# Keys of the first batch in halves, constants in an early gap, and the first token sums on VectorE

## The chip, the cores and the metric

The kernel runs on one core of one Trainium2 chip. The core has four engines that compute, each with its own queue of instructions in program order: TensorE (PE in the profile, its weight loads apart as PEld) multiplies matrices into PSUM, VectorE (DVE) and ScalarE (ACT) work on tiles in SBUF and PSUM, and GpSimd (POOL) works on tiles in SBUF alone. SyncE (SP) only issues transfers. The metric is device time in microseconds, the median over runs; one further execution is recorded by the profiler.

## The reference

The input x has eight batches of 1024 tokens with 512 features. A layer norm without weights gives xn. From it come two things that are multiplied and added back to x:

```python
xn = _layernorm(x)
s = concat([local, sparse, memory, prediction]) @ warboss_w + warboss_b
g = silu(relu(xn @ w1 + b1) @ w2 + b2)          # 512 -> 2048 -> 512
return x + s * g

# local:   softmax(q k^T * scale) v, one head of 128
# sparse:  the same, but a row keeps only its k_sparse = 102 largest of 1024 scores
#          (kth = top_k(scores)[..., -1]; where(scores >= kth, scores, -1e9))
# memory:  xp = xn @ memory_proj_w; weights = softmax(xp bank^T); [xp, weights bank] @ mem_out_w + b
# prediction: three linear layers, a gelu behind the second
```

All of it is in 32-bit floats.

## The kernel before, in words

A batch is cut into eight tiles of 128 tokens, four pairs, and two groups of 512 tokens. Token tiles are normalized with tokens in rows and turned by TensorE (`turn_tokens`, L328) into `xnT`, features in rows, one tile of 128 x 4 x 512 per group. For each tile of queries, `local` (L820) and `sparse` (L885) multiply the queries with the 1024 keys (`scores`, tile names `sc`), make a softmax, turn the probabilities (`ptp`) and, for a pair at a time, multiply with the values (`pa`). In `sparse` VectorE finds the 102nd largest score of each row in 13 rounds of MAX8 and MATCH_REPLACE8 (`sparse_select`, L850); ScalarE then scales the exponentials `es` by the reciprocal `r_s`.

The large products (both layers of the feed-forward, the two projections of the side heads, later queries and keys, and the output product) are made with seven block products where eight would be plain, as Strassen and Winograd do: sums of blocks of one operand (`t`, made from `xnT` in `token_sums`, L535; `hs` and `ho` from hidden values and heads), sums of blocks of the weights (`form_chunk`, L487), seven products, and sums of these (`u_...`, `m`). Weights are formed once, written back to DRAM and read from there afterwards.

The order of instructions on every engine is fixed when the kernel is built. `InOrder` (L77) chains each engine's instructions as the Python code issues them. The code keeps a model clock in units of TensorE columns (`clock`, L108): `run` (L133) looks through the chains, generators that yield the model time or the condition at which they may go on, takes the first that is ready, and otherwise issues one more multiplication of the feed-forward (`filler`, L662). `start` (L158) adds a chain with a rank. So a step that is issued at another place, or with another cost, shifts the model clock for what is behind it, and the planner may then order later steps in another way.

PSUM is shared by `ring` (L190): four buffers that are taken in turn; a buffer comes free when ScalarE has copied it out.

The change touches the first batch. `first_tokens` (L1043) normalizes eight tiles, two, two and four at a time, turns them, and makes the keys of the sparse head for one group of 512 tokens at a time (`project_k`, L342: four multiplications of 512 columns, one copy). After the first group come the first queries (`project_q`, L375), and three chains are started: `turn_constants` (L272), which turns the bias rows and the memory bank and multiplies the bank with half of `mem_out_w`; `token_sums` for group 0, four sums on GpSimd; and `hidden_sums`. Chunk 0 of the weights is formed by VectorE after the first four tiles are turned and the next four normalized. Then `sparse(0, 0)` multiplies the first scores; `run(needs(("sparse scores", 0)))` (L1071) waits for that, and queries of the second pair and the keys of the local head follow. From there a loop over 64 tiles sets the pace.

Of the kernel before, what the change touches and what calls it, by code (L numbers as in the profile page):

```python
# [15 lines left out]
P = 128  # L16
# [4 lines left out]
def kernel(  # L21
# [30 lines left out]
    NT = S // P  # L52
    NP = NT // 2
    NG = NT // 4
    T = 2 * P
    ND = D // P
# [7 lines left out]
    LOCAL, SPARSE = 0, 1  # L64
# [12 lines left out]
    class InOrder:  # L77
# [23 lines left out]
    pe, act, dve, pool, sp = (  # L101
        InOrder(e) for e in (nc.tensor, nc.scalar, nc.vector, nc.gpsimd, nc.sync)
    )
# [20 lines left out]
    def on(engine, columns):  # L124
        clock[engine] = max(clock[engine], clock["pe"]) + columns

    def after(engine, more=SLACK):
        return clock[engine] + more
# [29 lines left out]
    def start(generator, due=0, rank=1):  # L158
        chains.append([due, generator, rank])
        chains.sort(key=lambda c: c[2])  # L160

    def matmul(out, lhsT, rhs, start, stop, columns):
        pe.matmul(out, lhsT, rhs, start=start, stop=stop)
        tick(columns)

    def transpose(out, in_, ident):
        pe.transpose(out, in_, ident)
        tick(P // 2)

    def accumulate(ps, lhs, rhs, columns):  # L170
        n = len(lhs)
        for c in range(n):
            matmul(ps, lhs[c], rhs[c], c == 0, c == n - 1, columns)

    def copy(out, ps, columns):
        act.copy(out, ps)
        on("act", columns)

    def on_pool(op, out, in0, in1):
        getattr(pool, op)(out, in0, in1)  # L180
        n = 1
        for d in out.shape[1:]:
            n *= d
        on("pool", 60 + int(1.42 * n))

    def on_dve(op, out, in0, in1):
        getattr(dve, op)(out, in0, in1)
        on("dve", 340)

    def ring(name, shape):  # L190
        return ps_r.tile(list(shape), F32, tag="r", name=name)
# [32 lines left out]
    def borrow_qkv(name, which, tag="ws"):  # L224
        return borrow(name, *[w[:, which * HD : (which + 1) * HD] for w in qkv], tag=tag)
# [3 lines left out]
    first_k = borrow_qkv("wk_0", 1, "el")  # L229
    for h in range(2):  # L230
        t = sb.tile([P, 2, D], F32, tag="s", name=f"xl_0_{h}", bufs=2)
# [3 lines left out]
    first_q = borrow_qkv("wq_0", 0)  # L235
# [10 lines left out]
    for v in (ffn_b1, mem_out_b, pred_in_b, pred1_b, pred2_b):  # L246
        n = v.shape[0] // P
# [24 lines left out]
    def turn_constants():  # L272
        pt = ring("pt_b", (P, 4, P))
        transpose(pt[:, 0, :NB], brow, ident[:NB, :NB])
        transpose(pt[:, 1, :M], bank, ident[:M, :M])
        act.copy(biasT, pt[:, 0, :NB])
        copy(bankT[:, :M], pt[:, 1, :M], 300)
        yield after("act")
        pt = ring("pt_bm", (P, P))
        matmul(pt, bankT, w_mo[:, 1, :], True, True, HD)  # L280
        copy(bank_mo, pt, 200)
        done.add("constants")


    done = set()
    stats = {}
    xnT = {}
    qT = {}
    kT = {}
    vv = {}  # L290

    def needs(*keys):
        return lambda: all(k in done for k in keys)

    def ln_stats(b, j, t):
        if j == 0:
            mv = small.tile([P, NT, 2], F32, tag="mv", name=f"mv_{b}")
            rs = small.tile([P, NT], F32, tag="rs", name=f"rs_{b}")
            stats[b] = (mv, rs)
        st = small.tile([P, 6], F32, tag="st", name=f"st_{b}_{j}")  # L300
        dve.bn_stats(out=st, in_=t)
        dve.bn_aggr(out=stats[b][0][:, j, :], in_=st)
        on("dve", 540)
# [34 lines left out]
    def make_k(b):  # L338
        if b not in kT:
            kT[b] = sb.tile([P, 2, S], F32, tag="kT", name=f"kT_{b}")  # L340

    def project_k(b, g, h, w):  # L342

        make_k(b)
        ps = ring(f"pk_{b}_{g}_{h}", (P, 512))
        accumulate(
            ps,
            [w[:, c, ts(h, HD)] for c in range(ND)],
            [xnT[b, g][:, c, :] for c in range(ND)],
            512,  # L350
        )
        copy(kT[b][:, h, ts(g, 512)], ps, 360)
        done.add(("k", b, g, h))

    def project_v(b, q, w):

# [12 lines left out]
    def pair_xnT(b, p):  # L369
        return [xnT[b, p // 2][:, c, ts(p % 2, T)] for c in range(ND)]  # L370

    def make_q(b, p):
        qT[b, p] = sb.tile([P, 2, T], F32, tag="qT", name=f"qT_{b}_{p}", bufs=2)

    def project_q(b, p, w):  # L375

        make_q(b, p)
        ps = ring(f"pq_{b}_{p}", (P, 2, T))
        for h in range(2):
            accumulate(  # L380
                ps[:, h, :], [w[:, c, ts(h, HD)] for c in range(ND)], pair_xnT(b, p), T
            )
        act.activation(qT[b, p], ps, AF.Copy, scale=SCALE)
        on("act", 360)
        done.add(("q", b, p))
# [101 lines left out]
    def form_chunk(at):  # L487

        if at not in raw:
            return  # L490
        kind, n, k = order_of_chunks[at]
        what = raw.pop(at)
        w = w_tiles[kind, n, k]
        if what in ("down", "po"):
            on = on_pool if what == "down" else on_dve
            on("tensor_sub", w[:, 5], w[:, 3], w[:, 0])
            on("tensor_sub", w[:, 2], w[:, 6], w[:, 5])
            on("tensor_sub", w[:, 3], w[:, 6], w[:, 3])
            on("tensor_sub", w[:, 4], w[:, 1], w[:, 2])
        else:  # L500
            on_dve("tensor_add", w[:, 5], w[:, 3], w[:, 4])
            on_dve("tensor_sub", w[:, 2], w[:, 5], w[:, 0])
            on_dve("tensor_sub", w[:, 3], w[:, 0], w[:, 3])
            on_dve("tensor_sub", w[:, 6], w[:, 1], w[:, 2])
        sp.dma_start(out=w_dram[what, k], in_=w)
# [29 lines left out]
    def token_sums(g, name):  # L535

        b, q = divmod(g, NG)
        if g:
            yield needs(*[("xnT", b, 4 * q + j) for j in range(4)])
            yield after("act", 0)  # L540
        t = sb.tile([P, 4, 2, T], F32, tag="t", name=f"t_{name}")
        xs = xnT[b, q]
        b11, b12, b21, b22 = (xs[:, ts(h, 2), ts(j, T)] for h in range(2) for j in range(2))
        on_pool("tensor_sub", t[:, 0], b12, b11)
        on_pool("tensor_sub", t[:, 1], b22, t[:, 0])
        on_pool("tensor_sub", t[:, 2], b22, b12)
        on_pool("tensor_sub", t[:, 3], b21, t[:, 1])
        yield after("pool")
        tokens[g] = (b11, b21, t[:, 1], t[:, 2], t[:, 3], t[:, 0], b22)

    SLOTS = ((1, 4), (6, 5))
# [65 lines left out]
    def left_sums(h1, h2, s):  # L617


        a11, a21, a12, a22 = (h[:, ts(j, P)] for h in (h1, h2) for j in range(2))  # L620
        on_pool("tensor_add", s[:, 0], a21, a22)
        on_pool("tensor_sub", s[:, 1], s[:, 0], a11)
        on_pool("tensor_sub", s[:, 2], a11, a21)
        on_pool("tensor_sub", s[:, 3], a12, s[:, 1])
        return (a11, a12, s[:, 1], s[:, 2], a22, s[:, 0], s[:, 3])

    def hidden_sums():

        for _, n, k in [c for c in order_of_chunks if c[0] == "down"]:
            yield lambda: (n, k) in hidden and sums_made[0] < downs_made[0] + 3  # L630
            yield after("act", 0)
            h = hidden.pop((n, k))
            s = sb.tile([P, 4, P], F32, tag="hs", name=f"hs_{n}_{k}", bufs=3)
            operands[n, k] = left_sums(h[:, 0], h[:, 1], s)
            sums_made[0] += 1
            due = after("pool")
            wanted_at[n, k] = due
# [405 lines left out]
    def first_tokens():  # L1043
        def normalize_tokens(j0, j1):
            for j in range(j0, j1):
                ln_stats(0, j, first_x[j])
            ln_rstd(0, j0, j1)
            return [ln_apply(0, j, first_x[j]) for j in range(j0, j1)]

        due = normalize_tokens(0, 2) + normalize_tokens(2, 4)  # L1050
        for at in range(3):
            load_chunk(at)
        for g in range(NG):
            for j in range(4 * g, 4 * g + 4):
                yield due[j]
                turn_tokens(0, j, first_x[j])
            if g == 0:
                due += normalize_tokens(4, 8)
                form_chunk(0)
            yield after("act", 200)  # L1060
            project_k(0, g, SPARSE, first_k)
            if g == 0:
                project_q(0, 0, first_q)
                start(turn_constants())
                start(token_sums(0, 0), rank=0)
                start(hidden_sums(), rank=-1)

    STEP = int(0.995 * (11775 + NWC * (2 * 7 * T + 2 * 7 * H) // 4))
    start(first_tokens())
# [4 lines left out]
    for g in range(NG):  # L1074
        project_k(0, g, LOCAL, first_k)
# [3 lines left out]
    for n in range(B * NT):  # L1079
        b, i = divmod(n, NT)  # L1080
        p = i // 2
# [56 lines left out]
```

## Time and profile before

| | us |
|---|---|
| median of three runs | 2895.06 |
| the three runs | 2895.06, 2892.13, 2895.14 |
| the profiled execution's own time | 2892.31 |
| its span, first to last instruction | 2890.3 |
| TensorE busy | 2848.1 |
| VectorE busy | 2376.7 |
| GpSimd busy | 2187.9 |
| ScalarE busy | 1672.6 |
| mean granted TensorE clock | 0.997 |

The page gives busy time by engine, groups of instructions, and what ended the idle time before them. Further views show instructions in order of time (start, duration, engine, operation, output <- inputs, shapes, count; in brackets the idle time before and what ended it), who waited for whom, and the busy time of every engine in chosen stretches, in the order PE, PEld, DVE, ACT, POOL, with the clock that TensorE was granted (1.00 is full), the share of the transfer engines and GB/s. One 32-bit multiplication appears as two passes. Nearly all lines name L85, the helper that issues each instruction, so tile names tell steps apart.

### The profile page before, as it was taken

What the parts mean: (1) busy time and instruction counts of PE and PEld (TensorE: products, weight loads), DVE (VectorE), ACT (ScalarE), POOL (GpSimd) and SP (SyncE); (2) the same over time, 40 slices, a digit from 0 to 9 for tenths busy, and PEclk for the clock granted to TensorE, in tenths of its full rate; (3) what the DMA queues carried; (4) which work ended last, traced back from release to release, by engine and by line L of the source; (5) the groups of instructions that cost most, each with busy time, mean ns of one, the idle gap of its engine ahead of it and who ended that gap; (6) DMA issues with size and microseconds to landing.
All of it is one profiled execution on the core that took longest, in us unless ns stands there. A gap on an engine that the chain in (4) does not pass through costs nothing. (4 is left out here: it accounts for less than half of the span.)

```text
span 2890.3 us, 38499 instructions
## 1 busy us (share of the span) xinstructions
PE 2848.1 (99%) x13296; PEld 2394.5 (83%) x13296; DVE 2376.7 (82%) x3202; ACT 1672.6 (58%) x3174; POOL 2187.9 (76%) x2908
## 2 busy tenths in 40 slices
PE   8989999999999999999999999999999999999998
PEld 6878888888888888888888888888888888887887
DVE  7999979878698785988769897789967989588696
ACT  3546556665566654656546665556655556465564
POOL 4787867868678696786958879587796887867785
PEclk9999999999999999999999999999999999999999
DMA  5665644655455454454545545455455554544545
GB/s 179 215 243 193 209 160 160 223 179 205 148 178 214 175 201 162 172 213 163 206 165 186 206 177 193 164 204 199 156 196 184 186 203 169 197 146 174 200 168 187
DMA packets 132001, 538.89 MB, mean 186 GB/s; under 512 B 13790, under 2 KB 40432, under 8 KB 131808
## 3 DMA queue, kind: packets, MB, share of 16 engines
q1 hardware_dynamic: 126352, 519.23, 50.7%
q0 software_dynamic: 5456, 17.22, 1.6%
q8 instruction: 105, 1.72, 0.2%
q14 instruction: 88, 0.72, 0.1%
HBM read 500.35 MB, written 36.04 MB: 186 GB/s over the span
## 5 line engine op out<-in xcount | busy, mean ns | idle before, releaser
L85 DVE MAX8 top<-left 128x8 f32<-128x1024 f32 x768 | 943.2, 1228 | 26.7
L85 POOL TENSOR_TENSOR u_up<-u_up 128x256 f32<-128x256 f32 (+1 forms) x640 | 620.8, 976 | 318.7 <-ACT u_up L85 293.9
L85 DVE MATCH_REPLACE8 left<-top,left 128x1024 f32<-128x1024 f32 x704 | 850.6, 1208 | 0.0
L85 PE MATMUL f<-w_down,hs 128*128 128x256 f32 x2048 | 539.0, 380 | 2.1 <-POOL w_down L85 1.7
L85 PE MATMUL ph_up<-t,w_up 128*128 128x256 f32 x2048 | 483.3, 379 | 0.1
L85 PEld LDWEIGHTS f<-w_down,hs 128*128 128x128 f32 x2048 | 383.6, 191 | 61.5 <-issue 9.2
L85 PEld LDWEIGHTS ph_up<-t,w_up 128*128 128x128 f32 x2048 | 383.1, 190 | 60.2 <-issue 12.0
L85 PE MATMUL f<-w_down,h 128*128 128x256 f32 x1536 | 421.7, 380 | 3.4 <-ACT h L85 3.4
L85 ACT COPY u_up<-ph_up 128x512 f32<-128x512 f32 (+1 forms) x512 | 265.5, 531 | 237.8 <-PE ph_up L85 237.2
L85 PE MATMUL ph_up<-xnT,w_up 128*128 128x256 f32 x1536 | 383.1, 380 | 1.4 <-ACT u_up L85 0.9
L85 POOL TENSOR_TENSOR hs<-h 128x128 f32<-128x128 f32 x512 | 241.4, 471 | 171.2 <-PE f L85 135.7
L85 PEld LDWEIGHTS f<-w_down,h 128*128 128x128 f32 x1536 | 288.3, 191 | 50.7 <-issue 9.6
L85 PEld LDWEIGHTS ph_up<-xnT,w_up 128*128 128x128 f32 x1536 | 288.0, 190 | 48.8 <-issue 8.8
L85 PE MATMUL sc<-kT,qT 128*128 128x512 f32 x512 | 240.4, 593 | 0.2 <-ACT el L85 0.2
L85 PE MATMUL pa<-pT,v 128*128 128x256 f32 x1024 | 231.6, 379 | 0.0
L85 ACT ACTIVATE h<-u_up,biasT 128x256 f32<-128x256 f32 x512 | 220.2, 501 | 14.1 <-POOL u_up L85 14.1
L85 DVE TENSOR_REDUCE nml<-el 128x1 f32<-128x1024 f32 x64 | 77.3, 1208 | 181.0 <-ACT el L85 180.8
L85 PEld LDWEIGHTS pa<-pT,v 128*128 128x128 f32 x1024 | 194.4, 190 | 28.1 <-issue 1.0
L85 DVE MAX8 top<-s 128x8 f32<-128x1024 f32 x64 | 78.2, 1223 | 167.7 <-ACT s L85 167.5
L85 ACT COPY pT<-ptp 128x512 f32<-128x512 f32 x256 | 149.5, 588 | 113.7 <-PE ptp L85 113.1
L85 ACT ACT_TABLE_LOAD x139 | 178.3, 1283 | 5.0 <-DVE nms L85 2.0
L85 POOL TENSOR_TENSOR u_po<-u_po 128x256 f32<-128x256 f32 (+1 forms) x155 | 146.4, 951 | 19.8 <-ACT u_po L85 13.4
(151 smaller groups left out, 4574.7 us busy)
## 6 DMA issues: line engine op xcount, KB each, us to landing
w_down<-w_down_dram SPq DMA_DIRECT2D x248, 896.0 KB, 4.7
w_up<-w_up_dram SPq DMA_DIRECT2D x120, 896.0 KB, 4.6
w_po<-w_po_dram SPq DMA_DIRECT2D x62, 896.0 KB, 4.6
xl<-in_L_attn_x_dram SPq DMA_DIRECT2D x64, 256.0 KB, 4.8
xr<-in_L_attn_x_dram SPq DMA_DIRECT2D x64, 256.0 KB, 5.0
out_dram<-xr POOLq DMA_DIRECT2D x62, 256.0 KB, 3.0
xs<-in_L_attn_x_dram SPq DMA_DIRECT2D x56, 256.0 KB, 4.9
w_q<-w_q_dram SPq DMA_DIRECT2D x15, 896.0 KB, 4.6
```

The lines of the kernel that those rows point to most:

```text
L85: r = made(*args, **kwargs)
```

## The change

`project_k` can make a part of a group: with `parts=2` it multiplies 256 columns at a time and copies 256 columns of keys; the group counts as done with its last part. In `first_tokens` the loop goes over pairs of tiles, and a half projection follows each pair. `turn_constants` is no longer a chain of its own: its transposes are issued behind the first pair of tiles, its product behind the first half projection. The normalization of tiles 4 to 7 is issued behind that, the chains of token sums and hidden sums and the first queries behind the second pair, and chunk 0 is formed behind the third. `token_sums` issues group 0's four sums on VectorE, those of all other groups on GpSimd as before. The local head's keys and all other batches call `project_k` or make keys as before.

```diff
-    def project_k(b, g, h, w):
+    def project_k(b, g, h, w, part=0, parts=1):
 
         make_k(b)
-        ps = ring(f"pk_{b}_{g}_{h}", (P, 512))
+        n = 512 // parts
+        ps = ring(f"pk_{b}_{g}_{h}_{part}", (P, n))
         accumulate(
             ps,
             [w[:, c, ts(h, HD)] for c in range(ND)],
-            [xnT[b, g][:, c, :] for c in range(ND)],
-            512,
+            [xnT[b, g][:, c, ts(part, n)] for c in range(ND)],
+            n,
         )
-        copy(kT[b][:, h, ts(g, 512)], ps, 360)
-        done.add(("k", b, g, h))
+        copy(kT[b][:, h, ts(parts * g + part, n)], ps, 360 // parts)
+        if part == parts - 1:
+            done.add(("k", b, g, h))
...
-        on_pool("tensor_sub", t[:, 0], b12, b11)
-        on_pool("tensor_sub", t[:, 1], b22, t[:, 0])
-        on_pool("tensor_sub", t[:, 2], b22, b12)
-        on_pool("tensor_sub", t[:, 3], b21, t[:, 1])
-        yield after("pool")
+        on = on_pool if g else on_dve
+        on("tensor_sub", t[:, 0], b12, b11)
+        on("tensor_sub", t[:, 1], b22, t[:, 0])
+        on("tensor_sub", t[:, 2], b22, b12)
+        on("tensor_sub", t[:, 3], b21, t[:, 1])
+        yield after("pool" if g else "dve")
...
-        for g in range(NG):
-            for j in range(4 * g, 4 * g + 4):
+        constants = turn_constants()
+        for p in range(NT // 2):
+            g = p // 2
+            for j in range(2 * p, 2 * p + 2):
                 yield due[j]
                 turn_tokens(0, j, first_x[j])
-            if g == 0:
+            if p == 0:
+                next(constants)
+            yield after("act", 200)
+            project_k(0, g, SPARSE, first_k, p % 2, 2)
+            if p == 0:
+                next(constants, None)
                 due += normalize_tokens(4, 8)
+            elif p == 1:
+                start(token_sums(0, 0), rank=0)
+                project_q(0, 0, first_q)
+                start(hidden_sums(), rank=-1)
+            elif p == 2:
                 form_chunk(0)
-            yield after("act", 200)
-            project_k(0, g, SPARSE, first_k)
-            if g == 0:
-                project_q(0, 0, first_q)
-                start(turn_constants())
-                start(token_sums(0, 0), rank=0)
-                start(hidden_sums(), rank=-1)
```

## The prediction

> **What bounds the kernel now.** I read the page first, then the waits of TensorE, then its timeline at the start and around 160 to 185 us, then stretches of 3.4 us with the granted clock.
>
> ```profile
> span 2890.3 us, 38499 instructions
> ...
> PE 2848.1 (99%) x13296; PEld 2394.5 (83%) x13296; DVE 2376.7 (82%) x3202; ACT 1672.6 (58%) x3174; POOL 2187.9 (76%) x2908
> ```
>
> TensorE (PE) is busy for 99% of the span, and the change leaves its multiplications as they are. What can move is the rest: PE's waits (the view of waits adds to 32.8 us, 7.8 of them before the first instruction), half-clock stretches, and some 8 us after its last matmul. The start, PE's timeline:
>
> ```profile
> 7.79 1.94 PE L85 MATMUL ptx<-ident,xl 128*128 128x128 f32 x8 [7.79 <-DVE xl L85]
> 11.78 1.97 PE L85 MATMUL ptx<-ident,xl 128*128 128x128 f32 x8 [2.05 <-DVE xl L85]
> 14.42 5.49 PE L85 MATMUL pk<-xnT,wk 128*128 128x512 f32 x8 [0.68 <-ACT xnT L85]
> 19.75 3.62 PE L85 MATMUL pq<-xnT,wq 128*128 128x256 f32 x16
> ...
> 26.36 3.70 PE L85 MATMUL pk<-xnT,wk 128*128 128x512 f32 x8 [0.50 <-ACT xnT L85]
> ...
> 30.76 0.59 PE L85 MATMUL sc<-kT,qT 128*128 128x512 f32 x1
> ```
>
> See the idle 2.05, 0.68 and 0.50 us. The eight passes of the first key projection take 5.49 us, those of the second 3.70. The weight loads show why: their starts are 0.85 us apart until 18.0, then 0.43. TensorE runs at half rate up to about 18.3 us.
>
> ```profile
> 15.44 0.34 PEld L85 LDWEIGHTS pk<-xnT,wk 128*128 128x128 f32 x1 [0.52 <-issue]
> 16.29 0.34 PEld L85 LDWEIGHTS pk<-xnT,wk 128*128 128x128 f32 x1 [0.52 <-issue]
> ...
> 18.46 0.19 PEld L85 LDWEIGHTS pk<-xnT,wk 128*128 128x128 f32 x1 [0.24 <-issue]
> 18.89 0.19 PEld L85 LDWEIGHTS pk<-xnT,wk 128*128 128x128 f32 x1 [0.24 <-issue]
> ```
>
> VectorE's timeline, from the start to the first selection:
>
> ```profile
> 16.23 0.86 DVE L85 TENSOR_TENSOR sd<-rs 128x4 f32<-128x4 f32 x1
> 17.12 1.19 DVE L85 TENSOR_TENSOR sd<-sd,ve 128x4 f32<-128x4 f32 x1
> 18.34 1.20 DVE L85 TENSOR_SCALAR sd<-sd 128x4 f32<-128x4 f32 x1
> ...
> 33.29 1.23 DVE L85 MAX8 top<-s 128x8 f32<-128x1024 f32 x1 [8.68 <-ACT s L85]
> ...
> 48.78 1.22 DVE L85 TENSOR_REDUCE nml<-el 128x1 f32<-128x1024 f32 x1 [6.45 <-ACT el L85]
> ```
>
> Three four-column operations take 0.86 to 1.20 us while GpSimd adds the token sums (14.45 to 19.5); with two columns and GpSimd idle they take 0.16 to 0.24. VectorE then waits 8.68 and 6.45 us.
>
> The densest loss lies at 147 to 182 us. Columns of the stretches: busy time of each engine, then the clock:
>
> ```profile
> 161.60:165.00 3.40, 1.28 (x4) 0.76 (x5) 3.30 (x6) 1.88 (x4) 3.32 (x6) 0.98 1.03 378
> 165.00:168.40 3.40, 3.40 (x10) 2.71 (x10) 3.33 (x4) 1.11 (x2) 3.24 (x9) 0.52 0.54 222
> ...
> 175.30:178.70 3.40, 1.41 (x8) 0.77 (x7) 3.33 (x6) 2.52 (x5) 3.32 (x4) 0.97 0.00 0
> 178.70:182.10 3.40, 3.40 (x12) 2.82 (x11) 3.37 (x4) 2.03 (x5) 2.78 (x4) 0.53 0.29 84
> ...
> 2305.00:2308.40 3.40, 1.58 (x10) 1.11 (x9) 3.33 (x6) 1.21 (x2) 2.16 (x3) 1.00 0.77 270
> 2308.40:2311.80 3.40, 3.40 (x19) 3.01 (x18) 3.37 (x5) 3.38 (x8) 1.43 (x4) 1.00 0.00 0
> ```
>
> After a stretch with PE busy 1.28 or 1.41 us the next runs at half clock; after 1.58 it doesn't. So a wait of 2 us costs itself and about 1.7 more. The second such wait:
>
> ```profile
> 177.85 0.66 PE L85 MATMUL ptp<-ident,es 128*128 128x128 f32 x4 [1.99 <-ACT u_q L85]
> ```
>
> **The change part by part.** In the profiled execution work ahead of the first sparse scores (30.76) and behind them are added up separately.
>
> *Constants.* Two small transposes move from 24.17 to behind the second token transpose. Their biases land at 3.8 + 5.9 = 9.7 us and the memory bank at 4.3 + 6.2 = 10.5, so they end near 10.8, inside the idle time 9.73 to 11.78. The product with w_mo (landed at 11.4) follows the first half projection: some 0.3 us. About 0.6 us leave the later path.
>
> *Keys in halves.* The same columns run in 256-column passes (0.215 us each at full rate, 3.62 us by 16 in the pq row; 0.43 at half). First half: the copies of tiles 0 and 1 end at 11.10, so 11.15 to 14.57 at half rate. The w_mo product ends at 14.9. Tiles 2 and 3 (ready at 12.18) are now turned behind it, to 15.8 at full rate (eight take 0.87) or 16.6 at half. On ScalarE their copies stand behind the copies of kT (0.37) and bank_mo (0.28) and behind sd, which waits for VectorE until 15.75 and ends at 15.98; two copies of 1.07 together end at 17.05. Second half 17.1 to 18.8; queries to 22.25 (their weights landed at 16.6); tiles 4 and 5 to 23.1. Their copies stand behind qT and end at 24.1; half projection 24.15 to 25.87; tiles 6 and 7 to 26.73; three w_up matmuls (0.43 each) to 28.02, while the copies end at 27.55; last half to 29.74; two more w_up matmuls to 30.6. So the scores start 0.16 us earlier, with five w_up matmuls done instead of two: 3 x 0.43 = 1.29. Gain 1.45 us; bounds: 1.05 if tiles 2 and 3 are turned at half rate, 0 if every join costs 0.3 more, 2.0 if the clock opens a microsecond before 14.6. I take 1.45. Each added copy of 128x256 costs ScalarE 0.37, two of them more than before, beside idle time of 3.97 and 3.62 us at those places.
>
> *Token sums on VectorE.* GpSimd loses four sums of 1.26 us, and was idle behind them until 47.08, so that saves nothing there. The three slow operations fall to some 0.2, so tiles 4 to 7 are normalized at 18.97 instead of 21.69; PE comes to them at 22.25 anyway. The four sums cost VectorE 4 x 0.69 = 2.8 (its 128x512 row at the end of the kernel), to 21.7, and the forms of chunks 0 and 1 (3.01) end at 24.7; without the 8.68 us wait they would be on the path to the first MAX8. First use of a sum or formed block: about 30 us. The write of formed chunk 0 on SP's queue, with the loads of w_m behind it, starts up to 1.5 us later; w_m is used at 66 us and later.
>
> *What moves behind.* The order of instructions of the changed kernel forms chunk 2 before the 48.78 reduction: 3.47 us of work goes into the 6.45 us wait. This lead ends at tile 1, whose scores come when they did, and about 0.35 us is left. GpSimd is packed from 130.4 to 163.4 (hs, forms of w_down, ho, u_up) with the same list in both orders, started by PE at w_down 2, which comes 1.45 earlier: the waits of 1.67, 1.08, 2.29 and 0.39 and the first half-clock stretch move along, at no gain. At 177.85 the order differs: five more matmuls stand ahead of the transposes, and the copy of ph_q that held the buffer stands ahead of es. PE would come at 175.86 - 1.45 + 5 x 0.43 = 176.56. The reciprocal behind the second MAX8 of tile 3 ends at 176.14 - 0.35 = 175.8, es 1.15 later at 176.95. The wait falls from 1.99 to 0.4: 1.6 us (bounds 0 and 2.0). Then PE is busy for about 3.0 of the 3.4 us, above 1.58, and the half-clock stretch 178.7 to 182.1 goes: 1.7 us (bounds 0 and 1.7).
>
> [...]
>
> Sum: 1.45 + 1.6 + 1.7 = 4.75 us. The profiled execution's own time is 2892.31 (span 2890.3 and 2.0 around it), so 2887.6; the median shown is 2895.06, 2.75 above it, and against that **2890.3 us**.
>
> Later, 14.1 us of waits and one half-clock stretch are spread over 369 to 2881 us, five of them of 1.75 to 2.23 us, where transposes of probabilities meet ScalarE at a table load or VectorE at a reciprocal. The order shifts by a few instructions throughout, so these fall anew. Runs of over 3.3 us on ScalarE without a copy out of PSUM number 30 before and 29 after. I take no change, and 4.3 us either way (five long waits of 1.9 us, give or take the root of five).
>
> **The rivals.** (1) *The later waits fall well*: two or more of the five long ones missing, 2890.3 - 3.8 = 2886.5 and below; nothing speaks for or against it but that the order is new.
> (2) *Slower: PE meets VectorE's selection.* For each sparse tile I counted PE's work from scores to transposes (matmuls x 0.43 or 0.86) less VectorE's (rounds of 2.55 us and what lies between), copies and scaling. Under 2 us are left in 9 of 64 tiles before, in 18 after, and in the last tile -0.1 instead of 3.6. If each of the nine new ones waits 1.8 us, that is +16: 2906. It breaks even at three and passes 0.2% (5.8 us, about what a measurement can tell from no change) at six. Against it: PE's waits at transposes of sparse probabilities before, at 650, 1205, 2308 and 2658 us, fall in none of the nine tight tiles.
> (3) *The clock opens later, so the start gains nothing.* Before, it opened 3.9 us after the work became unbroken (14.42 to 18.3). Now a pause of transposes and waits at 14.9 to 17.1 breaks it. If that starts the count anew, it opens at 21.0; 3.9 us at half rate lose 1.95: 2892.3. For it: the transposes at 11.78 did not open it. Against it: 11.15 to 14.9 is unbroken nearly as long. [...]
> (4) *The rearrangement does nothing*: the tile-2 wait stays at 2 us with its stretch: 2893.6.
>
> **How the numbers follow.** Forecast 0.48, its own range 2887 to 2893, with 0.19 of it under 2889.3; rival 1 0.24; rival 2 0.14; 3 and 4 together 0.14. Faster by over 0.2%: 0.19 + 0.24 = 0.43; within: 0.29 + 0.14 = 0.43; slower: 0.14. The range 2882 to 2901 adds the 4.3 us of later waits and the bounds on either side, and leaves out most of rival 2 and the far end of rival 1.
>
> **What would show it.** Right: keys in passes of 256 from 11.2 us, sc at 30.6 with ten w_up passes ahead, tile-4 normalization near 17, clock 1.00 throughout 172 to 185, and waits of PE near 31 us. Wrong: half-rate passes at 17 to 21 us, a wait over 1 us at the tile-2 transposes, or waits at es totalling well over 6 us in the later batches.

## The result: 9 us faster, twice the sum, and by another way

The changed kernel takes **2885.6 us** (median of 7 runs, 2883.36 to 2887.35) against 2895.06 (7 runs, 2892.13 to 2896.72): a ratio of 0.9968, 95% interval 0.9958 to 0.9978, so 9.4 us or 0.32% faster. That lies inside the range of the prediction and outside the 2887 to 2893 of its likeliest case. The profiled executions differ less, 2890.3 to 2883.6 us of span; single runs of one kernel lie up to 6 us apart (2884.02 to 2890.42 us in one of the experiments). Two lines of the page of the changed kernel:

```profile
span 2883.6 us, 38540 instructions
...
PE 2844.9 (99%) x13312; PEld 2397.6 (83%) x13312; DVE 2381.0 (83%) x3206; ACT 1674.4 (58%) x3175; POOL 2184.2 (76%) x2904
```

TensorE is busy for 99% as before (16 passes more, since two passes of 256 columns stand for one of 512). PE's timeline at the start of the changed kernel:

```profile
11.77 3.73 PE L85 MATMUL pk<-xnT,wk 128*128 128x256 f32 x8 [1.37 <-ACT xnT L85]
...
17.44 1.99 PE L85 MATMUL pk<-xnT,wk 128*128 128x256 f32 x8 [0.84 <-ACT xnT L85]
...
27.24 1.46 PE L85 MATMUL ph_up<-xnT,w_up 128*128 128x256 f32 x6
...
30.27 0.59 PE L85 MATMUL ph_up<-xnT,w_up 128*128 128x256 f32 x2
30.70 0.59 PE L85 MATMUL ph_up<-t,w_up 128*128 128x256 f32 x2
31.13 1.88 PE L85 MATMUL sc<-kT,qT 128*128 128x512 f32 x4
```

In the kernel before, one group of w_up passes stands ahead of the scores at 30.76 us:

```profile
29.89 1.03 PE L85 MATMUL ph_up<-xnT,w_up 128*128 128x256 f32 x4
```

The keys run in halves and the second half already at full rate (1.99 us for eight passes). The scores start 0.37 us later than before, but behind ten w_up passes instead of four; six passes are 1.29 us, so the start leads by 0.92 us.

The same timeline where the prediction saw the denser gain:

```profile
162.25 1.22 PE L85 MATMUL f<-w_down,h 128*128 128x256 f32 x2 [4.73 <-ACT h L85]
...
178.42 0.66 PE L85 MATMUL ptp<-ident,es 128*128 128x128 f32 x4 [2.12 <-ACT es L85]
```

The wait at the transposes of tile 2 is still there, 2.12 us for 1.99, and a new one of 2.07 us comes at 189.88, at w_po. Counted over 60 to 300 us, PE waits 10.0 us instead of 7.7. From 300 us on it is the other way round. PE's waits of the changed kernel there (total, times, longest), 9.0 us in all:

```profile
PE ptp L85 <- ACT u_up L85: 2.4, 1, 2.4
PE ptx L85 <- ACT u_up L85: 2.0, 1, 2.0
PE ptx L85 <- ACT u_po L85: 1.0, 1, 1.0
PE sc L85 <- ACT u_po L85: 0.9, 1, 0.9
PE ptx L85 <- DVE xl L85: 0.9, 2, 0.6
PE ph_up L85 <- ACT u_up L85: 0.8, 1, 0.8
PE ptp L85 <- ACT es L85: 0.7, 2, 0.5
PE f L85 <- ACT m L85: 0.3, 1, 0.3
```

The kernel before has 14.1 us in the same stretch:

```profile
PE ptp L85 <- ACT u_up L85: 4.7, 3, 2.2
PE ptp L85 <- ACT es L85: 3.8, 3, 1.8
PE ptp L85 <- ACT el L85: 2.0, 1, 2.0
PE ptx L85 <- DVE xl L85: 1.6, 3, 0.7
PE ph_up L85 <- ACT u_up L85: 0.9, 1, 0.9
PE ptp L85 <- ACT u_k L85: 0.5, 1, 0.5
...
```

So of the 6.7 us between the two profiles 5.1 are waits behind 300 us, hundreds of microseconds behind the last edited instruction. The lead of the start is gone before that. At 193.86 us both kernels begin the same passes (`f<-w_down,h`), and TensorE has done the same work up to there, but for eight transposes (`ptp<-ident,el`, 0.87 us), which only the kernel before has behind it. So the changed kernel is 0.9 us behind at that point. Counted pass by pass (0.43, 0.216 and 0.109 us for 512, 256 and 128 columns at full clock) it is still 0.2 us behind at 300 us. The whole gain falls behind 300 us: 5 us of it are waits, and some 2 us are neither waits in the view nor half-clock stretches.

The expectation of the first experiment below speaks of 1.0 us won by 200 us. That figure came from busy time that is left at 200 us (2665.7 us, and 2666.7 in the kernel before). Busy time is not work: the same work takes 2848.1 us of it in one kernel and 2844.9 in the other.

### The profile page after: what moved, and what is told of

Read it like the earlier page. It is cut to its first block, busy times and chain, and to the rows that moved or that the text cites. A ratio compares the mean times of both kernels' runs of the same rounds, so it can differ in the third digit from the quotient of the medians.

```text
span 2883.6 us, 38540 instructions
## 1 busy us (share of the span) xinstructions
PE 2844.9 (99%) x13312; PEld 2397.6 (83%) x13312; DVE 2381.0 (83%) x3206; ACT 1674.4 (58%) x3175; POOL 2184.2 (76%) x2904
```

## The experiments

*Head* means here the start of the first batch, up to the regular steps of the loop, and *order* the sequence in which the planner puts everything behind it. There are two theories. *Order (O)*: the planner starts its regular steps 2000 columns behind its own clock at the end of the head; the change moves that clock against the filler, so that everything behind the head is interleaved anew, and the new order happens to hold fewer waits. *Head (H)*: the gain is made in the head and carried to the end.

The number 2000 (`begin`) gives the tool. With it the later order can be chosen apart from the head. Built with starts from 800 to 3200 in steps of 100 and compared instruction by instruction, the old head gives the order of the kernel before only at 2000; at 2100 to 2500, and again at 2900, TensorE's last 6300 instructions (of some 7300 listed) are those of the changed kernel. The new head gives the old order at 1100 and 1200 and the new one at 1300 to 2000. The border has moved by some 800 columns; the three w_up matmuls more that fit ahead of the scores are 768.

**Both orders with the other head, and parts alone.** First the new head with the token sums back on GpSimd, which falls into the old order by itself:

```diff
-        on = on_pool if g else on_dve
-        on("tensor_sub", t[:, 0], b12, b11)
+        on_pool("tensor_sub", t[:, 0], b12, b11)
...
-        yield after("pool" if g else "dve")
+        yield after("pool")
```

> The new head (keys in halves, constants in the first gap) with the token sums back on GpSimd. With that one term returned, the planner falls back into the old order: VectorE, GpSimd and the DMA queue take the same instructions in the same order as in the kernel before, and TensorE does from the first w_up passes on. If the gain is made in the order behind the head (theory O: the profiled pair had won 1.0 us by 200 us and 5.7 us behind it), this kernel keeps only the head's 0.9 to 1.5 us: 2893.5 to 2895. If the gain is the head's own and is carried to the end (theory H), it keeps it nearly all: 2885 to 2888.

Measured: 2893.31 us, ratio 1.0000 (0.9991 to 1.0008). Not even the head's 0.9 us came: in this head, with the token sums on GpSimd, the planner puts no more filler ahead of the scores than before. They start at 30.80 us behind four w_up passes, as in the kernel before, and PE waits 0.78 and 0.72 us for copies of the tokens at the last two half projections. By 369 us (the transposes at u_k, 371.71 for 369.51) this kernel is 2.2 us behind.

The reverse, the old head with the new order:

```diff
-    begin = clock["pe"] + 2000
+    begin = clock["pe"] + 2200
```

> The head of the kernel before, untouched; only the start of the regular steps is put 200 columns of the planner's clock later (2200 for 2000). With it the planner falls into the order of the changed kernel: from the fifth w_up passes of the third group on TensorE takes its last 6373 instructions in the same order as the changed kernel, and the other engines do likewise. Theory O: 2886 to 2888.5. Theory H: 2894 to 2896, as nothing of the change is in it.

Measured: 2887.44 us, ratio 0.9980 (0.9971 to 0.9989). Nothing of the change is in this kernel, and it has 5.5 us of the gain. PE's waits behind 300 us in it:

```profile
PE ptp L85 <- ACT u_up L85: 2.4, 1, 2.4
PE ptx L85 <- ACT u_up L85: 2.0, 1, 2.0
PE ptx L85 <- ACT u_po L85: 1.0, 1, 1.0
PE sc L85 <- ACT u_po L85: 0.9, 1, 0.9
PE ptx L85 <- DVE xl L85: 0.9, 2, 0.5
PE ph_up L85 <- ACT u_up L85: 0.8, 1, 0.8
PE ptp L85 <- ACT es L85: 0.6, 2, 0.4
PE f L85 <- ACT m L85: 0.3, 1, 0.3
```

Line by line these are the changed kernel's, to 0.1 us. The waits belong to the order.

Keys in halves alone (`project_k` as in the change, not shown again):

```diff
-        for g in range(NG):
-            for j in range(4 * g, 4 * g + 4):
+        for p in range(NT // 2):
+            g = p // 2
+            for j in range(2 * p, 2 * p + 2):
...
-            if g == 0:
+            if p == 1:
...
-            project_k(0, g, SPARSE, first_k)
-            if g == 0:
+            project_k(0, g, SPARSE, first_k, p % 2, 2)
+            if p == 1:
                 project_q(0, 0, first_q)
                 start(turn_constants())
```

> Keys in halves alone; the constants stay a chain of their own and the token sums GpSimd's, the second batch of normalization and the first forms stand where they stood. The planner falls into the changed kernel's order from the third group on. Theory O: 2885 to 2888, the same as the changed kernel. Theory H: the halves hold the larger part of the head's 1.45 us, the rest of the gain is missing: 2892 to 2894.

Measured: 2886.68 us, ratio 0.9976 (0.9967 to 0.9985), as O said. At 43.2 us its PE leads the kernel before by 0.45 us; the rest of its 6 us is the order, with 8.9 us of waits behind 300 us. Eight w_up passes stand ahead of its scores (four at 27.59 us, four at 30.31), though the token sums are GpSimd's.

The token sums alone:

```diff
-        on_pool("tensor_sub", t[:, 0], b12, b11)
+        on = on_pool if g else on_dve
+        on("tensor_sub", t[:, 0], b12, b11)
...
```

> Only the first token sums are VectorE's. TensorE, ScalarE and the DMA queue take exactly the instructions of the kernel before in their order. Theory O: no change, 2894 to 2896. Theory H: GpSimd has four sums less at the start, so its jam at 130 to 163 us could end earlier; the four waits there (1.67, 1.08, 2.29 and 0.39 us) would fall and the time would be 2890 to 2893.

Measured: 2892.24 us, ratio 0.9999 (0.9990 to 1.0008): nothing, and PE's four waits at 147 to 165 us stand as they were (1.65, 1.08, 2.26, 0.40).

The constants alone:

```diff
+        constants = turn_constants()
         for g in range(NG):
             for j in range(4 * g, 4 * g + 4):
                 yield due[j]
                 turn_tokens(0, j, first_x[j])
+                if j == 1:
+                    next(constants)
+                elif j == 3:
+                    next(constants, None)
...
-                start(turn_constants())
```

> Only the constants are turned in TensorE's first gap, between the transposes of tiles 1 and 2, with the product of the memory bank behind tile 3; keys and token sums as before. The order behind the keys is the old one on every engine. Theory O: 2892 to 2895, no change. Theory H, by the step of the prediction that gave the gap 0.5 us of the keys' way to the scores: 0.5 us less at the first scores and as much at the end, 2892 to 2894, which the medians can't tell from O; the profile can: the first scores at 30.3 us instead of 30.8, and the lead there or gone at the waits of 147 to 190 us.

Measured: 2891.2 us, ratio 0.9998 (0.9989 to 1.0008). The scores did start at 30.10 us, but the whole start was early: the first transposes began at 7.16 us for 7.79, so only 0.03 us of it is the edit's. PE's timeline shows where the rest went:

```profile
22.90 1.91 PE L85 MATMUL ptx<-ident,xl 128*128 128x128 f32 x16
25.70 3.70 PE L85 MATMUL pk<-xnT,wk 128*128 128x512 f32 x8 [0.89 <-ACT xnT L85]
```

The transposes run through without the constants between them, and PE then waits 0.89 us for ScalarE's copies of the last tiles where it had waited 0.50 behind the constants. The constants had been standing in a gap already.

**The changed kernel whole, in the old order.**

```diff
-    begin = clock["pe"] + 2000
+    begin = clock["pe"] + 1150
```

> The changed kernel whole, token sums on VectorE too, with the start at 1150 for 2000, which brings the old order back from the second batch on: TensorE's last 6321 instructions are those of the kernel before, in its order. Theory O: the waits behind 600 us are those of the kernel before (0.6, 2.2, 2.0, 0.7, 0.9, 1.8, 1.75 and 1.8 us at the same instructions) and the time is 2890 to 2895, of which what falls short of 2893 is the first batch's. Theory H: 2884 to 2888.

Measured: 2891.54 us, ratio 0.9994 (0.9985 to 1.0003). The long waits of the kernel before are back at the same instructions. Four of its lines, which have 2.23, 2.02, 1.75 and 1.84 us in the kernel before as well:

```profile
649.72 0.66 PE L85 MATMUL ptp<-ident,es 128*128 128x128 f32 x4 [2.23 <-ACT u_up L85]
...
1074.35 0.66 PE L85 MATMUL ptp<-ident,el 128*128 128x128 f32 x4 [2.02 <-ACT el L85]
...
2629.26 0.66 PE L85 MATMUL ptp<-ident,el 128*128 128x128 f32 x4 [1.75 <-ACT u_up L85]
2655.93 0.66 PE L85 MATMUL ptp<-ident,es 128*128 128x128 f32 x4 [1.84 <-ACT es L85]
```

**Other orders.** If an order is a draw, that is, chance as far as anyone planned it, others should scatter whatever the head. Two with the old head (the second has 1800 in the same place):

```diff
-    begin = clock["pe"] + 2000
+    begin = clock["pe"] + 1000
```

> The kernel before with the regular steps begun at 1000 columns of the planner's clock instead of 2000: its head, and a third order of the instructions behind it, neither that of the kernel before nor that of the changed one. Theory O says that an order is a draw and the head no part of it: the waits of TensorE behind 300 us, 14.0 us in the old order and 9.1 in the new, come out anew anywhere from 6 to 20 us, and the time between 2884 and 2900, whichever head it has. Theory H: 2892 to 2896, as for the kernel before.

> The kernel before with the start at 1800 for 2000: the old head and a fourth order. Theory O: a draw, 2884 to 2900, with the waits behind 300 us and 1.7 us for each stretch at half the clock making up the difference from the kernel before to within 2 us. Theory H: 2892 to 2896.

Measured: 2885.96 us (0.9971, 0.9960 to 0.9982) and 2883.45 us (0.9966, 0.9953 to 0.9979), with 6.8 and 5.2 us of waits behind 300 us. Both are about as fast as the changed kernel or faster, with one number altered in the kernel before. The new head at 2600:

> The changed kernel with the start at 2600 for 2000: the new head and a fifth order. Theory O: a draw, 2884 to 2900, no better placed than the old head's orders. Theory H: the changed kernel's time, 2884 to 2888, since the head is the same to the instruction.

Measured: 2881.85 us, ratio 0.9960 (0.9946 to 0.9975), 5.3 us of late waits: below the changed kernel, whose head it shares. It lies some 2 us below both expected ranges, as the start at 1800 lay 0.6 us below theory O's. Once more:

> The kernel of the run with the new head and the start at 2600 once more, with more rounds, since it is the fastest so far (2881.85 us). An order is fixed when the kernel is built, so theory O says that its time and its waits come again: 2880.5 to 2883.5, with 5.3 us of waits behind 300 us at the same instructions, and the rest of the spread is half-clock stretches of 1.7 us. If the low time was chance of the run and not of the order, it moves towards the mean of all orders, 2886 to 2890.

Measured: 2881.16 us, ratio 0.9955 (0.9942 to 0.9969), 5.2 us of late waits, the same six groups as in the run before it. This is the fastest kernel found. And one more of each head:

> The changed kernel with the start at 3000 for 2000: new head, a further order. Theory O: a draw between 2880 and 2894 with TensorE's waits behind 300 us at 5 to 14 us; the span less those waits and less 1.7 us for each stretch at half the clock behind 300 us is 2872 to 2877, as it is in every kernel so far (2872.5 to 2877.1).

> The kernel before with the start at 3100 for 2000: old head, a further order. Theory O as for the one beside it: a draw between 2880 and 2894, and the span less the late waits and 1.7 us a half-clock stretch again at 2872 to 2877. If the head were worth the 9 us, no order of the old head would come below 2888; two have already.

Measured: 2893.53 us (1.0003, 0.9994 to 1.0013) for the new head and 2886.95 us (0.9979, 0.9970 to 0.9988) for the old. The first settles it against H: the changed kernel's head, and no gain at all. The second half of what I expected failed: the span less late waits and late half-clock stretches is 2880.2 and 2878.8, not 2872 to 2877. The first batch has its draw too. PE's waits of the new head at 3000, from 60 to 300 us, 14.4 us for the changed kernel's 10.0:

```profile
PE ptp L85 <- ACT es L85: 6.4, 1, 6.4
PE f L85 <- ACT h L85: 3.2, 1, 3.2
PE pa L85 <- ACT u_up L85: 2.5, 1, 2.5
...
```

All kernels together. Waits of PE and stretches at half the clock are those of the profiled executions; a stretch is 3.41 us long, and they are counted from 60 us to the last matmul.

| head | order | time, us | ratio to before | waits 60-300 | waits behind 300 | half-clock stretches |
|---|---|---|---|---|---|---|
| old | old (before) | 2895.06 | 1 | 7.7 | 14.1 | 3 |
| token sums only | old | 2892.24 | 0.9999 | 7.6 | 15.2 | 2 |
| constants only | old | 2891.2 | 0.9998 | 8.8 | 14.0 | 1 |
| new, sums on GpSimd | old | 2893.31 | 1.0000 | 9.5 | 14.0 | 4 |
| new | old from batch 2 | 2891.54 | 0.9994 | 10.7 | 13.7 | 2 |
| new | new (after) | 2885.6 | 0.9968 | 10.0 | 9.0 | 4 |
| halves only | new | 2886.68 | 0.9976 | 10.3 | 8.9 | 4 |
| old | new | 2887.44 | 0.9980 | 10.1 | 8.9 | 4 |
| old | start 1000 | 2885.96 | 0.9971 | 12.0 | 6.8 | 2 |
| old | start 1800 | 2883.45 | 0.9966 | 11.9 | 5.2 | 2 |
| old | start 3100 | 2886.95 | 0.9979 | 13.4 | 5.7 | 3 |
| new | start 2600 | 2881.85 | 0.9960 | 9.9 | 5.3 | 3 |
| new | start 2600 again | 2881.16 | 0.9955 | 11.9 | 5.2 | 4 |
| new | start 3000 | 2893.53 | 1.0003 | 14.4 | 8.6 | 5 |

The kernel before was measured anew beside the experiments, at 2892.84 to 2894.22 us, so ratios are to be compared, not times; a ratio is the recorded one against the kernel before of the same session, over all runs, and not the quotient of two medians of this table. Of seven orders the old one is among the two slowest: the change had much to gain by leaving it, by any way. At one order, the head is worth 0 to 0.12% (new order: 0.9968 and 0.9976 against 0.9980; old order: 0.9994 and 1.0000 against 1), which these intervals of 0.1% either way don't tell from nothing.

## Why the prediction came out as it did

**The number was near and the likeliest mechanism was not.** Of its three terms one holds in part. What carried the result is the sentence on the later waits, "I take no change, and 4.3 us either way", and with it rival 1. Nothing spoke for the later waits to fall well, so that they did was luck. The prediction's own sign of being wrong came too: a wait of over 1 us at the tile-2 transposes.

- *Head, 1.45 us: the mechanism holds, the size was 0.92.* Halves, clock, fillers and the ten passes came as told, with scores at 31.13 for 30.6. The normalization of the first two tiles took longer in this execution (1.78 us for 1.18), so that the first half started at 11.77 and not 11.15. The lead does not last: at 193.86 us the changed kernel is 0.9 us behind the kernel before, as shown above. Against the old head in the new order little of it is left: at the token transposes of 573 us, the same instruction in the same order, the changed kernel is at 573.46 and the old head with the new order at 573.66, a lead of 0.20 that had been 0.70 at 43 us.
- *Constants, 0.6 us off the later path: wrong.* Alone they gave 0.03; the copies behind them are late instead.
- *Token sums: as told.* The three small operations fell to 0.16 and 0.17 us, and the normalization of tiles 4 to 7 began at 17.46 and ended at 19.38 (18.97 was forecast). Alone they moved nothing. In the changed head they decide how far the filler runs ahead of the scores: four w_up passes with the sums on GpSimd, ten with them on VectorE.
- *GpSimd's jam moves along at no gain: right in its sum.* Waits of 1.67, 1.08, 2.29 and 0.39 (5.4 us) became 1.08 and 4.73 (5.8 us).
- *Tile 2, 1.6 us: wrong.* PE came at 176.30, as worked out (176.56). The reciprocal did not: 175.8 was forecast, from a lead of 0.35 us kept by VectorE. VectorE's timeline of the changed kernel:

```profile
82.40 1.23 DVE L85 MAX8 top<-s 128x8 f32<-128x1024 f32 x1 [0.40 <-ACT s L85]
...
115.20 0.69 DVE L85 BATCH_NORM_STATS2 st<-xs 128x6 f32<-128x512 f32 x1 [1.20 <-DMA xs<-in_L_attn_x_dram]
...
134.50 1.28 DVE L85 SCALAR_TENSOR_TENSOR es<-s,top,es 128x1024 f32<-128x1024 f32 x1
...
177.04 0.14 DVE L85 RECIPROCAL r_s<-tots 128x1 f32<-128x1 f32 x1
```

  Before, the reciprocal was at 176.00, so VectorE is 1.04 us late instead of early. At the end of tile 0's selection it was still 0.11 us early (80.51 for 80.62); at the end of tile 1's it is 1.65 us late (134.50 for 132.85). Between these two points VectorE does the same 73 instructions in both kernels, with 51.3 and 51.2 us of busy time, but it is idle for 2.65 us instead of 1.05. The two waits in the lines above, for ScalarE's copy of tile 1's scores and for the landing of tokens (`xs`), are not in the kernel before, and the prediction had neither. Why that transfer landed later is open: it was issued at 108.70 us, for 108.99 before.
- *Half-clock stretch at tile 2, 1.7 us: wrong with it.* The stretches of 3.4 us in the changed kernel; the second column is PE's busy time, the one after the engines the clock:

```profile
158.50:161.90 3.40, 0.00 (x0) 0.00 (x0) 3.33 (x6) 0.22 (x1) 3.24 (x5) 0.53 1.00 411
161.90:165.30 3.40, 3.06 (x7) 2.09 (x8) 3.30 (x5) 1.79 (x4) 3.24 (x8) 0.50 1.06 401
...
176.00:179.40 3.40, 1.28 (x7) 0.95 (x7) 3.37 (x5) 2.18 (x4) 3.19 (x4) 0.97 0.26 74
179.40:182.80 3.40, 3.40 (x12) 2.73 (x12) 3.30 (x6) 2.02 (x4) 1.70 (x2) 0.53 0.00 0
```

  There are three half-clock stretches up to here, before there were two; in the first of the three TensorE had nothing to do (0.00 us busy), so it cost nothing. The relation behind the term holds at tile 2: 1.28 us busy, then half the clock. The prediction's border between 1.41 and 1.58 us is not a sharp one, as the last section shows.
- *Not foreseen: w_po at 189.88.* VectorE begins its last forms of w_po at 188.93, and PE came for them at 187.81 (189.88 less the wait). In the kernel before the forms began at 187.74, PE came to the same group of passes at 188.67, and it didn't wait.
- *Rival 2, tight selections:* fell. Transposes of sparse probabilities waited 3.1 us in all behind 300 us and 7.0 in the kernel before, so 3.9 less and not 16 more; counting tight tiles from the order did not forecast a wait.
- *Rival 3, a later clock:* fell. The clock's first record at full begins at 15.32 us (before: at 18.06), behind the first half projection and ahead of the pause that the rival reckons with. The eight transposes at 15.56 us take 1.04 us, where the first eight, at 7.80, took 2.08. So this run does not test whether a pause starts the count anew.
- *Rival 4, nothing at all:* right for tile 2, wrong for the total.

What stays open: behind 300 us neither passes at full clock, PE's waits nor half-clock stretches account for 12.0 to 12.5 us in the profiles of the old order and of the new head's start at 3000, and for 9.7 to 10.7 us in all others. Where these 2 us come from, I could not find.

## What to carry to other kernels

Where a planner interleaves the work, an edit at the start is two edits: its own, and a new draw of the whole order behind it. Before crediting a gain of some tenths of a per cent to the edit, build the old code with the new order and the new code with the old one; here one start offset did both, and gave a kernel of 2881 us besides. A gain worked out in the head is worth its price only if the next full engine (here GpSimd at 147 to 165 us, then VectorE's selections) does not take it back.

## What the runs showed of the hardware

Waits that an order makes repeat to a few hundredths of a microsecond from kernel to kernel (2.23, 2.02, 0.72, 0.86, 1.75 us at the same instructions in the kernels of the old order; one of them, token sums only, has a wait of 1.16 us more, at 1044.66). What differs more is the half-clock stretch behind them. The changed kernel, then the old head in the new order, at the same instruction:

```profile
1005.77 0.66 PE L85 MATMUL ptx<-ident,xl 128*128 128x128 f32 x4 [1.97 <-ACT u_up L85]
1006.26 1.98 PE L85 MATMUL sc<-kT,qT 128*128 128x512 f32 x4
1008.08 1.03 PE L85 MATMUL ph_up<-xnT,w_up 128*128 128x256 f32 x4
```

```profile
1005.99 0.66 PE L85 MATMUL ptx<-ident,xl 128*128 128x128 f32 x4 [1.97 <-ACT u_up L85]
1006.48 2.90 PE L85 MATMUL sc<-kT,qT 128*128 128x512 f32 x4
1009.17 1.84 PE L85 MATMUL ph_up<-xnT,w_up 128*128 128x256 f32 x4
```

The same wait of 1.97 us is followed by full clock in one and by half in the other, where the next two groups take 2.90 and 1.84 us for 1.98 and 1.03. By the transposes of 1715 us the second kernel has fallen back by 1.7 us (708.97 against 710.66 us between the two places), which is the price of one stretch.

The recorded clock tells the two apart. In the changed kernel's record a half-clock stretch lasts 3.413 us, the first one behind 60 us twice that (it counts as two). Behind 60 us the stretches of these two executions begin whole multiples of 3.413 us apart: at 158.69, 179.16 and 1715.16 us in the changed kernel (6 and 450 times), at 160.89, 1007.40 and 1717.37 us in the other (248 and 208 times). Cut in steps of this length from there, the wait of the changed kernel lies over two steps, with PE busy for 2.02 and 2.84 us, and the wait of the other kernel in one, with 1.44. The second column is PE's busy time, the one after the engines the clock:

```profile
1001.78:1005.19 3.41, 2.02 (x10) 1.44 (x8) 0.00 (x0) 3.39 (x7) 0.39 (x1) 1.00 0.00 0
1005.19:1008.61 3.42, 2.84 (x11) 1.76 (x12) 0.00 (x0) 2.79 (x7) 2.84 (x3) 1.00 0.02 5
```

```profile
1003.99:1007.40 3.41, 1.44 (x7) 0.91 (x7) 0.00 (x0) 3.28 (x7) 2.38 (x2) 1.00 0.00 0
1007.40:1010.82 3.42, 3.42 (x7) 2.00 (x6) 0.79 (x1) 1.66 (x3) 1.03 (x3) 0.50 0.02 5
```

The step with 1.44 us is followed by half the clock (0.50), those with 2.02 and 2.84 us by full clock. What sets the marks was not shown: no run here moved them by themselves. Cut in this way from 60 us to 12 us before the end, the full-clock steps that half the clock follows have PE busy for 1.11, 1.43 and 1.39 us in the kernel before (from 161.42, 175.07 and 1072.78 us) and for 1.16, 1.29 and 1.01 us in the changed kernel (from 155.27, 175.75 and 1711.75 us). The least busy ones that full clock follows have 1.57 us in the kernel before (from 2656.57 us) and 1.81 us in the changed one (from 185.99 us). In two other runs: 1.50 us at 217.38 in the run with the old head and the start at 1800, then full clock; 1.76 us at 144.23 in the run with the constants alone, then half. So half the clock followed 1.76 us in one run and full clock 1.50 us in another.
